# State-space stages: decays and convolution kept in PSUM, masked products on VectorE, between-block products issued together

## The chip, the cores and the metric

The kernel runs on one core of a Trainium2 chip. The core has five engines with queues of their own: TensorE (PE, matrix products into PSUM), VectorE (DVE), ScalarE (ACT, functions such as Exp and Silu), GpSimd (POOL) and SyncE (SP, which here issues transfers). The metric is the time of one execution on the device in microseconds; lower is better. Three executions before the change took 3060.55, 3071.86 and 3084.89 us.

## The reference

The program is a decoder of four layers on x of 16 rows x 128 positions x 256 features. Every layer adds three stages to x, each fed by a layer norm of x: an attention-like stage, a cross attention to a context, and a feed-forward stage. The change touches the first stage of layers 1 and 2, which are state-space stages. Cut to what matters, with L1 having 4 heads of 128 and a state of 64, L2 32 heads of 16 and a state of 128:

```python
zxbcdt = norm(x) @ W_in                      # gate z, xBC, dt
xBC = silu(causal_conv(xBC, taps=4) + bias)  # 512 + 2 * state channels
X, B, C = split(xBC)
dt = softplus(dt + dt_bias)                  # L2: clipped at 0
a = dt * -exp(A_log)                         # per position and head
G[l, s] = C[l] . B[s]
decay[l, s, h] = exp(sum of a[k, h], s < k <= l) for s <= l, else 0
y[l, h] = sum over s of G[l, s] * decay[l, s, h] * dt[s, h] * X[s, h] + D[h] * X[l, h]
y = y * silu(z)
x = x + (y * rsqrt(mean(y * y) + 1e-5) * norm_w) @ W_out
```

The reference writes the sum over s in chunks (64 positions in L1, 32 in L2), with a state carried between chunks; it is the same sum. The factor of the decay between two chunks splits into three: from s to the end of its chunk, over the chunks between, and from the start of l's chunk to l.

## The kernel before

`mamba` (line 761) computes both stages. `L1_attn` and `L2_attn` (992, 995) call it; `blocks` (767) is true for L2 alone. The 16 rows are handled in four groups of four (`NG`, `GB`).

`project(g)` (822) makes the group's projections. The channels lie on the partitions, the four rows' 512 positions beside each other. For each of six channel chunks it makes `pconv` in a PSUM bank, copies it with ACT into `xp` in SBUF (832, with three zero columns ahead of each row, set by POOL), writes the last tap and the bias with ACT into `xc` or `bc` in SBUF (834), adds the other three taps there with three DVE instructions (836), and applies Silu in place with ACT (839). It yields after every second chunk, so that its caller can interleave it. The rest of it, after the third yield, makes the gate `sz` (four chunks `pz`), `dt` with a softplus of many small DVE instructions, `a`, and in L2 the factors `xy` between chunks: three that go to the sources (already multiplied by `dt`) and one that goes to the result.

`begin(g, j)` (874) starts one row. It transposes X into `xs` with positions on the partitions, multiplies `xc` by D on POOL (881), makes `pg`, which is G, and `gm`, which is G with the causal mask (L2: with the mask inside a chunk of 32 alone). For the decays, DVE makes `rb` (894), PE sums it into `pseg`, and ACT writes its Exp to `lc` in SBUF (903): one tile of 512 columns in L1, two in L2. In L2 it goes on with the products between chunks: ACT copies G into `gf` (912); for each chunk c = 1, 2, 3, POOL makes `xw` from the 32, 64 or 96 positions before it (917), and PE multiplies the matching corner of `gf` with it into 32 partitions of the bank `poff` (923). The first 32 partitions get a product with a tile of zeros, `none` (922). DVE scales the result to `yo` (925).

`parts` (930, L2) finishes the row within chunks: POOL makes `xdp` (X times `dt`, even and odd heads apart), eight products `mt` of a decay with `gm` are made, five on DVE and three on POOL (939), PE multiplies each into `py` (946) in four columns of 32, and adds `yo` by a product with the identity (950). `whole` (953, L1) does the same with one `mt`. `gate` (961) adds to `xc` on DVE, multiplies by `sz` on POOL and squares on ACT; `out` (968) makes the mean, `rms` and the output product `po`, and adds to x.

The order is written by hand at the end of `mamba` (980 to 990) with `Pipe` (line 124), a list of work with the number of steps until it is due:

```python
for j in range(GB):
    begin(g, j, *ready[g])
    pipe.step()
    for _ in range((0, 2, 1, 9)[j]):
        next(work, None)
```

`begin` puts `parts` or `whole` two steps ahead, so a row's second half follows the `begin` of the next row; `gate` puts `out` one step ahead. Then comes a piece of the next group's projection: none in the pass of the first row, two pieces (four conv chunks) in the second, one in the third, and the rest in the fourth. The framework sets the waits and lays each engine's queue in about this order; where an instruction's operands are late in its planning, it can put later work ahead. On the chip each queue runs in the order so laid.

Tiles come from pools with a fixed number of buffers for each tag. PSUM has eight banks: four in the pool `mm` (`pconv`, `pz`, `pxy`, `pseg`, `poff`), two in `tp` (transposes, `pg`, `prms`, `po`) and two in `ac` (`py`, `pdt`).

Of the kernel before, what the change touches and what calls it, by code (L numbers as in the profile page):

```python
# [11 lines left out]
F32 = mybir.dt.float32  # L12
# [4 lines left out]
AF = mybir.ActivationFunctionType  # L17
ALU = mybir.AluOpType
# [4 lines left out]
P = 128  # L23
NB = 16
S = 128
D = 256
GB = 4
# [14 lines left out]
class Decoder:  # L42
# [718 lines left out]
    def mamba(self, L, H, N, clip):  # L761
# [3 lines left out]
        nc = self.nc  # L765
        HD, Q = 512 // H, 32
# [6 lines left out]
        with ExitStack() as es:  # L773
            pool = lambda n, b: es.enter_context(self.tc.tile_pool(name=L + n, bufs=b))
            one, ap, cv, sm, big = pool("1", 1), pool("a", 2), pool("cv", 2), pool("sm", 2), pool("big", 3)
            cw = one.tile([P, 6, 5], F32, tag="cw", name="cw")
# [11 lines left out]
            if blocks:  # L788
                g_ = nc.gpsimd
                tl = lambda n, k=P: one.tile([P, k], F32, tag=n, name=n)  # L790
                b4 = lambda t: t.rearrange("p (b i) -> p b i", b=4)

                after, upto, turn = tl("afterb"), tl("uptob"), tl("upto32", Q)
                for t, whole in ((after, self.after), (upto, self.upto)):
                    g_.affine_select(
                        out=b4(t), in_=b4(whole), pattern=[[-Q, 4], [0, Q]], compare_op=ALU.is_ge, fill=0.0, base=0,
                        channel_multiplier=1,
                    )
                    g_.affine_select(
                        out=b4(t), in_=b4(t), pattern=[[Q, 4], [0, Q]], compare_op=ALU.is_ge, fill=0.0, base=Q - 1,  # L800
                        channel_multiplier=-1,
                    )
                nc.vector.tensor_reduce(turn, upto.rearrange("p (b i) -> p i b", b=4), AX.X, ALU.add)

                rest = []
                for c in range(1, 4):
                    t = tl(f"rest{c}")
                    g_.affine_select(
                        out=t, in_=self.after, pattern=[[0, P]], compare_op=ALU.is_ge, fill=0.0, base=Q * c - 1,
                        channel_multiplier=-1,  # L810
                    )
                    rest.append(t)
                none = one.tile([Q, Q], F32, tag="none", name="none")
                g_.memset(none, 0.0)

                xds = [one.tile([P, H // 2, 64], F32, tag=f"xdp{i}", name=f"xdp{i}") for i in range(2)]
                for t in xds:
                    g_.memset(t, 0.0)
            else:
                after, upto = self.after, self.upto  # L820

            def project(g):
                xT = self.norm_T(g)
                xc = cv.tile([P, 4, GB, S], F32, tag="xc", name="xc")
                bc_ = ap.tile([P, 2, GT], F32, tag="bc", name="bc")
                for c, (at, m) in enumerate(CH):
                    pm = self.psum("pconv")
                    self.chain(pm[:m], [(w[:, k, at : at + m], xT[:, k, :]) for k in range(2)])
                    pj = pm[:m].rearrange("p (j s) -> p j s", j=GB)
                    xp = cv.tile([P, GB, S + 3], F32, tag="xp", name="xp")  # L830
                    nc.gpsimd.memset(xp[:m, :, 0:3], 0.0)
                    nc.scalar.copy(xp[:m, :, 3:], pj)
                    acc = xc[:m, c] if c < 4 else bc_[:m, c - 4, :].rearrange("p (j s) -> p j s", j=GB)
                    nc.scalar.activation(acc, pj, AF.Identity, bias=cw[:m, c, 4:5], scale=cw[:m, c, 3:4])  # L834
                    for k in range(3):
                        nc.vector.scalar_tensor_tensor(  # L836
                            acc, xp[:m, :, k : k + S], cw[:m, c, k : k + 1], acc, ALU.mult, ALU.add
                        )
                    nc.scalar.activation(acc, acc, AF.Silu)
                    if c % 2:  # L840
                        yield
                sz = ap.tile([P, 4, GT], F32, tag="sz", name="sz")
                for c in range(4):
                    pz = self.psum("pz")
                    self.chain(pz, [(wz[:, k, self.cols(c)], xT[:, k, :]) for k in range(2)])
                    nc.scalar.activation(sz[:, c, :], pz, AF.Silu)
                dt = ap.tile([P, GB, H], F32, tag="dt", name="dt")
                a = ap.tile([P, GB, H], F32, tag="a", name="a")
                flat = lambda t: t.rearrange("p j h -> p (j h)")
                pd = self.psum_a("pdt")[:, : GB * H].rearrange("p (j h) -> p j h", j=GB)  # L850
                for j in range(GB):
                    self.chain(pd[:, j, :], [(xT[:, k, self.cols(j)], w[:, k, DT : DT + H]) for k in range(2)])
                nc.vector.tensor_tensor(dt, pd, dtb.unsqueeze(1).broadcast_to([P, GB, H]), ALU.add)
                self.softplus(sm, flat(dt))
                if clip is not None:
                    nc.vector.tensor_scalar(dt, dt, clip[0], clip[1], ALU.max, ALU.min)
                nc.vector.tensor_tensor(a, dt, A.unsqueeze(1).broadcast_to([P, GB, H]), ALU.mult)
                xy = None
                if blocks:

                    px = self.psum("pxy")
                    for c in range(4):
                        nc.tensor.matmul(px[:, self.cols(c)], rest[c] if c < 3 else upto, flat(a), start=True, stop=True)
                    xy = ap.tile([P, 4, GB, H], F32, tag="xy", name="xy")
                    nc.scalar.activation(xy.rearrange("p c j h -> p (c j h)"), px, AF.Exp)
                    nc.vector.tensor_tensor(
                        xy[:, 0:3].rearrange("p c j h -> p c (j h)"), xy[:, 0:3].rearrange("p c j h -> p c (j h)"),
                        flat(dt).unsqueeze(1).broadcast_to([P, 3, GB * H]), ALU.mult,
                    )
                ready[g] = bc_, sz, xc, dt, a, xy  # L870
# [3 lines left out]
            def begin(g, j, bc_, sz, xc, dt, a, xy):  # L874
# [17 lines left out]
                for u in range(H // per):  # L892
# [6 lines left out]
                    )  # L899
                    ps = self.psum("pseg")  # L900
                    nc.tensor.matmul(ps, after, rb.rearrange("p h l -> p (h l)"), start=True, stop=True)
                    lc = big.tile([P, per, U], F32, tag="lc", name="lc", bufs=4)
                    nc.scalar.activation(lc.rearrange("p h l -> p (h l)"), ps, AF.Exp)
                    lcs.append(lc)
                if not blocks:
                    xd = sm.tile([P, 512], F32, tag="xd", name="xd")
                    nc.gpsimd.tensor_tensor(heads(xd), heads(xs), dj, ALU.mult)
                    pipe.put(2, lambda: whole(g, j, gm, lcs[0], xd, sz, xc))
                    return
                xd = xds[b % 2]  # L910
                gf = sm.tile([P, P], F32, tag="gf", name="gf")
                nc.scalar.copy(gf, pg[:, :P])
                pf = self.psum("poff")
                for c in range(1, 4):
                    n = Q * c
                    xw = big.tile([P, 512], F32, tag="xw", name="xw")
                    nc.gpsimd.tensor_tensor(
                        heads(xw)[:n], heads(xs)[:n],
                        xy[:n, c - 1, j, :].unsqueeze(2).broadcast_to([n, H, HD]), ALU.mult,
                    )  # L920
                    if c == 1:
                        nc.tensor.matmul(pf[0:Q], none, xw[0:Q], start=True, stop=True)
                    nc.tensor.matmul(pf[n : n + Q], gf[:n, n : n + Q], xw[:n], start=True, stop=True)
                yo = sm.tile([P, 512], F32, tag="yo", name="yo")
                nc.vector.tensor_tensor(
                    heads(yo), heads(pf), xy[:, 3, j, :].unsqueeze(2).broadcast_to([P, H, HD]), ALU.mult
                )
                pipe.put(2, lambda: parts(g, j, gm, lcs, xd, dj, yo, xs, sz, xc))

            def parts(g, j, gm, lcs, xd, dj, yo, xs, sz, xc):  # L930
                for e in range(2):
# [2 lines left out]
                py = self.psum_a("py")  # L934
                for c in range(4):
                    for e in range(2):
                        mt = big.tile([P, 4, 4, Q], F32, tag="mt", name="mt", bufs=3)
                        at = 8 * (c % 2) + e
                        (nc.gpsimd if e and c else nc.vector).tensor_tensor(  # L939
                            mt,  # L940
                            lcs[c // 2][:, at : at + 7 : 2, :].unsqueeze(2).broadcast_to([P, 4, 4, Q]),
                            gm.rearrange("p (b l) -> p b l", b=4).unsqueeze(1).broadcast_to([P, 4, 4, Q]),
# [40 lines left out]
            for g in range(NG):  # L983
                work = iter(project(g + 1)) if g + 1 < NG else iter(())
                for j in range(GB):
                    begin(g, j, *ready[g])
                    pipe.step()
                    for _ in range((0, 2, 1, 9)[j]):
                        next(work, None)
            pipe.drain()  # L990

    def L1_attn(self):
# [699 lines left out]
```

## Time and profile before

| | us |
|---|---|
| profiled execution | 3070.78 |
| its span on the core | 3069.1 |
| median of the three runs | 3071.86 |
| PE busy | 2517.6 (82%) |
| DVE busy | 1684.7 (55%) |
| POOL busy | 937.2 (31%) |
| ACT busy | 877.0 (29%) |

A profile is of one execution. A row of a group names line, engine and operation, the tile written and the tiles read, their shapes, and how many there were; then the busy time of the group in us and the mean of one in ns; then the idle time of the engine ahead of it and what ended it. A row of the busy table by stretches gives the stretch, its length, and the busy us of each engine with the number of instructions, then the mean granted clock of PE, the share of the transfer engines and their GB/s. A row of the timeline begins with start and length in us. A row of waits gives engine and line that waited, what it waited for, the us in total, how often, and the longest. A float32 matrix product shows as two instructions.

L1_attn fills about 643 to 840 us of the span and L2_attn about 1224 to 1625 us, with their neighbours overlapping at the edges.

### The profile page before, as it was taken

The numbers are of one execution on the slowest core, as the hardware profiler recorded it, in microseconds if no ns is written. First come the engines' busy times: TensorE is split into PE (matmuls) and PEld (weight loads), VectorE is DVE, ScalarE is ACT, GpSimd is POOL, SyncE is SP. The second block draws the span as 40 slices with busy tenths as digits, with TensorE's granted clock in tenths as the row PEclk, the third lists the DMA queues.
The fourth block names the chain that finished last, engine by engine and source line by source line (L and its number), as shares of the span: only waits on it lengthen the run. The fifth ranks groups of instructions, "written<-read, shape, count | busy, mean of one in ns | idle before, by whom it ended". The sixth has DMA issues, their size and how long they took to land. (4 is left out here: it accounts for less than half of the span.)

```text
span 3069.1 us, 33079 instructions
## 1 busy us (share of the span) xinstructions
PE 2517.6 (82%) x12524; PEld 1571.2 (51%) x12524; DVE 1684.7 (55%) x3219; ACT 877.0 (29%) x1602; POOL 937.2 (31%) x953
## 2 busy tenths in 40 slices
PE   7214998999879888889989888759998986888986
PEld 4102444556534555344445555525765565676665
DVE  6998894257643676866776666562145554211110
ACT  1002544135444311423313333221114430111111
POOL 3452111014520122444566666400023324011121
PEclk9556889999968999977889999969888985899998
DMA  4000001000100001000000000010000011132121
GB/s 121 0 0 23 24 6 42 0 31 1 39 14 1 1 1 35 4 1 1 5 20 7 1 1 1 26 42 0 24 13 1 13 54 61 51 95 64 55 75 14
DMA packets 58141, 74.33 MB, mean 24 GB/s; under 512 B 7620, under 2 KB 49669, under 8 KB 57878
## 3 DMA queue, kind: packets, MB, share of 16 engines
q1 hardware_dynamic: 50678, 63.66, 6.6%
q0 software_dynamic: 7296, 8.48, 1.5%
q8 instruction: 101, 1.65, 0.2%
q14 instruction: 66, 0.54, 0.1%
HBM read 55.12 MB, written 18.04 MB: 24 GB/s over the span
## 5 line engine op out<-in xcount | busy, mean ns | idle before, releaser
L1578 POOL DMA_INDIRECT out_dram<-y,xe x40 | 62.0, 1549 | 382.7 <-ACT y L1577 293.7
L1569 DVE TENSOR_TENSOR hT<-sl,pgb 128x320 f32<-128x320 f32 x112 | 54.6, 488 | 195.3 <-PE pgb L92 195.3
L230 PE MATMUL pt<-ident,o 128*128 128x128 f32 x64 | 18.7, 362 | 156.2 <-POOL o L298 132.7
L92 PE MATMUL pga<-xeT,e_w1T 128*128 128x320 f32 x448 | 143.2, 443 | 0.0
L92 PE MATMUL pgb<-xeT,e_w3T 128*128 128x320 f32 x448 | 139.7, 434 | 0.0
L92 PE MATMUL pa<-e_w2T,hT 128*128 128x256 f32 x560 | 125.9, 384 | 0.0
L549 DVE TENSOR_TENSOR hT<-sl,pgb 128x512 f32<-128x512 f32 (+1 forms) x56 | 38.5, 688 | 142.3 <-PE pgb L92 134.9
L92 PEld LDWEIGHTS pa<-e_w2T,hT 128*128 128x128 f32 x560 | 107.3, 193 | 14.9
L195 POOL COPY rs<-mv 128x4 f32<-128x4 f32 x48 | 11.4, 237 | 320.6 <-DVE mv L194 320.6
L1313 POOL TENSOR_TENSOR sc<-sc,mx 128x512 f32<-128x512 f32 x64 | 65.2, 1039 | 136.8 <-DVE mx L1312 99.2
L939 DVE TENSOR_TENSOR mt<-lc,gm 128x512 f32<-128x512 f32 x80 | 100.0, 1266 | 9.9 <-PE py L946 8.8
L92 PEld LDWEIGHTS pga<-xeT,e_w1T 128*128 128x128 f32 x448 | 87.3, 197 | 35.4 <-issue 1.8
L92 PEld LDWEIGHTS pgb<-xeT,e_w3T 128*128 128x128 f32 x448 | 86.0, 192 | 36.3 <-issue 1.4
L1568 ACT ACTIVATE sl<-pga 128x320 f32<-128x320 f32 x112 | 49.0, 437 | 191.3 <-PE pga L92 191.3
L270 POOL TENSOR_TENSOR prod<-qkv 128x2048 f32<-128x2048 f32 (+7 forms) x24 | 86.5, 3609 | 48.4 <-DVE o L294 28.7
L198 DVE TENSOR_SCALAR xn<-x,mv,rs 128x256 f32<-128x256 f32 x192 | 83.5, 484 | 25.6 <-POOL rs L102 25.6
L230 PEld LDWEIGHTS pt<-ident,o 128*128 128x128 f32 x64 | 9.1, 164 | 171.4 <-POOL o L298 139.8
L92 PE MATMUL pconv<-xT,w_L_w 128*128 128x512 f32 (+1 forms) x192 | 93.1, 631 | 0.7 <-ACT xT L84 0.5
L620 PE MATMUL ps<-qb,kn 32*128 32x256 f32 x512 | 88.7, 524 | 4.0 <-DVE kn L606 2.8
L382 PE MATMUL ps<-qb,kT 32*128 32x512 f32 x256 | 80.3, 714 | 13.6 <-ACT pT L387 10.4
L836 DVE SCALAR_TENSOR_TENSOR xc<-xp,cw,xc 128x512 f32<-128x512 f32 x96 | 84.1, 906 | 12.8 <-ACT xc L834 10.0
L1120 ACT ACTIVATE sc<-sc 128x512 f32<-128x512 f32 x64 | 40.3, 630 | 162.1 <-POOL sc L1119 162.1
(473 smaller groups left out, 6331.8 us busy)
## 6 DMA issues: line engine op xcount, KB each, us to landing
e_w1T<-in_L_w1T SPq DMA_DIRECT2D x8, 896.0 KB, 6.2
e_w3T<-in_L_w3T SPq DMA_DIRECT2D x8, 896.0 KB, 6.5
e_w2T<-in_L_w2T SPq DMA_DIRECT2D x8, 896.0 KB, 6.3
slots<-blank SPq DMA_DIRECT2D x8, 652.5 KB, 11.2
xe<-slots SPq DMA_DIRECT2D x8, 652.5 KB, 4.1
ct<-in_ctx SPq DMA_DIRECT2D x8, 512.0 KB, 5.4
x<-in_x SPq DMA_DIRECT2D x4, 512.0 KB, 6.2
ctx<-in_ctx SPq DMA_DIRECT2D x16, 128.0 KB, 2.2
```

The costliest lines, as they stand in the source:

```text
L92: self.nc.tensor.matmul(out, a, b, start=(i == 0), stop=(i == n - 1))
L198: nc.vector.tensor_scalar(xn[:, j, :], self.x[:, g * GB + j, :], mv[:, j, 0:1], rs[:, j : j + 1], ALU.subtract, ALU.mult)
L270: nc.gpsimd.tensor_tensor(prod[:, :k, :], qkv[:, m0 : m0 + k, 256:512], q, ALU.mult)
L382: nc.tensor.matmul(ps[r], kT[rw, j, c, :], qb[rw, j, c].rearrange("p e n -> p (e n)"), start=True, stop=True)
L620: nc.tensor.matmul(ps[r][:, D * c : D * c + D], kn[rw, j, self.cols(c)], qb[rw, j, e], start=True, stop=True)
L836: nc.vector.scalar_tensor_tensor(acc, xp[:m, :, k : k + S], cw[:m, c, k : k + 1], acc, ALU.mult, ALU.add)
L939: (nc.gpsimd if e and c else nc.vector).tensor_tensor(mt, lcs[c // 2][:, at : at + 7 : 2, :].unsqueeze(2).broadcast_to([P, 4, 4, Q]), gm.r ...
L1120: nc.scalar.activation(sc, sc, AF.Exp, scale=scale)
L1313: nc.gpsimd.tensor_tensor(sc, sc, mx.unsqueeze(2).broadcast_to([P, 4, S]), ALU.add)
L1568: nc.scalar.activation(sl, pa[:, :HALF], AF.Silu)
L1569: nc.vector.tensor_tensor(hT[:, f, hs], sl, pb[:, :HALF], ALU.mult)
L1578: nc.gpsimd.indirect_dma_start(out, bass.IndirectOffsetOnAxis(xe[:, t, D + 4 : D + 5].bitcast(I32), 0), y, None, bounds_check=NB * S - 1, ...
```

## The change

All of it is in `mamba`:

- The convolution stays in `pconv`'s PSUM bank: ACT writes the last tap and the bias there in place, DVE adds the three other taps there, and Silu alone writes `xc` or `bc` in SBUF.
- The Exp of the decays is written in place into `pseg`'s bank. There is no `lc` tile; `mt` reads the bank.
- All eight `mt` of a row in L2 are made on DVE, with five buffers instead of three.
- `gf` is made on DVE as G times a mask `prior` that is one for pairs of different chunks alone, so that the corners need not be cut: each `xw` has 96 positions (four buffers instead of three), and the four products into `poff` are issued one after the other, all with 96 rows; the first chunk's product takes the first `xw` and masked zeros. The tile `none` goes.
- `begin` returns the row's second half instead of putting it into the pipe. The loop calls it after the piece of projection of the same pass.

```diff
-                none = one.tile([Q, Q], F32, tag="none", name="none")
-                g_.memset(none, 0.0)
+                prior = tl("prior")
+                nc.vector.tensor_tensor(prior, self.upto, upto, ALU.subtract)
...
-                    acc = xc[:m, c] if c < 4 else bc_[:m, c - 4, :].rearrange("p (j s) -> p j s", j=GB)
-                    nc.scalar.activation(acc, pj, AF.Identity, bias=cw[:m, c, 4:5], scale=cw[:m, c, 3:4])
+                    nc.scalar.activation(pj, pj, AF.Identity, bias=cw[:m, c, 4:5], scale=cw[:m, c, 3:4])
                     for k in range(3):
                         nc.vector.scalar_tensor_tensor(
-                            acc, xp[:m, :, k : k + S], cw[:m, c, k : k + 1], acc, ALU.mult, ALU.add
+                            pj, xp[:m, :, k : k + S], cw[:m, c, k : k + 1], pj, ALU.mult, ALU.add
                         )
-                    nc.scalar.activation(acc, acc, AF.Silu)
+                    to = xc[:m, c] if c < 4 else bc_[:m, c - 4, :].rearrange("p (j s) -> p j s", j=GB)
+                    nc.scalar.activation(to, pj, AF.Silu)
...
-                    lc = big.tile([P, per, U], F32, tag="lc", name="lc", bufs=4)
-                    nc.scalar.activation(lc.rearrange("p h l -> p (h l)"), ps, AF.Exp)
-                    lcs.append(lc)
+                    nc.scalar.activation(ps, ps, AF.Exp)
+                    lcs.append(ps.rearrange("p (h l) -> p h l", h=per))
...
-                    pipe.put(2, lambda: whole(g, j, gm, lcs[0], xd, sz, xc))
-                    return
+                    return lambda: whole(g, j, gm, lcs[0], xd, sz, xc)
...
-                nc.scalar.copy(gf, pg[:, :P])
-                pf = self.psum("poff")
-                for c in range(1, 4):
-                    n = Q * c
-                    xw = big.tile([P, 512], F32, tag="xw", name="xw")
+                nc.vector.tensor_tensor(gf, pg[:, :P], prior, ALU.mult)
+                pf, n, xws = self.psum("poff"), 3 * Q, []
+                for c in range(3):
+                    xw = big.tile([P, 512], F32, tag="xw", name="xw", bufs=4)
                     nc.gpsimd.tensor_tensor(
-                        heads(xw)[:n], heads(xs)[:n],
-                        xy[:n, c - 1, j, :].unsqueeze(2).broadcast_to([n, H, HD]), ALU.mult,
+                        heads(xw)[:n], heads(xs)[:n], xy[:n, c, j, :].unsqueeze(2).broadcast_to([n, H, HD]), ALU.mult
                     )
-                    if c == 1:
-                        nc.tensor.matmul(pf[0:Q], none, xw[0:Q], start=True, stop=True)
-                    nc.tensor.matmul(pf[n : n + Q], gf[:n, n : n + Q], xw[:n], start=True, stop=True)
+                    xws.append(xw)
+                for c in range(4):
+                    to = slice(Q * c, Q * c + Q)
+                    nc.tensor.matmul(pf[to], gf[:n, to], xws[max(c - 1, 0)][:n], start=True, stop=True)
...
-                pipe.put(2, lambda: parts(g, j, gm, lcs, xd, dj, yo, xs, sz, xc))
+                return lambda: parts(g, j, gm, lcs, xd, dj, yo, xs, sz, xc)
...
-                        mt = big.tile([P, 4, 4, Q], F32, tag="mt", name="mt", bufs=3)
+                        mt = big.tile([P, 4, 4, Q], F32, tag="mt", name="mt", bufs=5)
                         at = 8 * (c % 2) + e
-                        (nc.gpsimd if e and c else nc.vector).tensor_tensor(
+                        nc.vector.tensor_tensor(
...
-                    begin(g, j, *ready[g])
+                    rest_of = begin(g, j, *ready[g])
                     pipe.step()
                     for _ in range((0, 2, 1, 9)[j]):
                         next(work, None)
+                    rest_of()
```

## The prediction

> **What bounds the kernel now.** The page's chain of waits covers only the last 35 us of the run, so it tells nothing here. I read the busy table by stretches first. The change touches two stages: L1_attn, whose steady part is 660 to 835 us, and L2_attn, 1256 to 1622 us.
> ```profile
> core 0: us, PE busy (x) PEld busy (x) DVE busy (x) ACT busy (x) POOL busy (x), PEclk, DMA share, GB/s
> 660.00:835.00 175.00, 160.65 (x715) 105.85 (x714) 125.45 (x269) 89.64 (x134) 72.84 (x88) 0.93 0.03 8
> 1256.00:1622.00 366.00, 327.73 (x1911) 165.55 (x1910) 263.84 (x350) 106.93 (x167) 204.25 (x197) 0.83 0.02 7
> ```
> PE is busy 90% of L2_attn and 92% of L1_attn; DMA is nothing. L2_attn has 16 batch rows at 366/16 = 22.9 us each, at a granted clock of only 0.83. So PE leads, with DVE (72%) behind. Next the groups of DVE and POOL within L2_attn, and what PE waited for:
> ```profile
> L939 DVE TENSOR_TENSOR mt<-lc,gm 128x512 f32<-128x512 f32 x80 | 100.0, 1266 | 9.9 <-PE py L946 8.8 <-DVE mt L939 0.3
> L836 DVE SCALAR_TENSOR_TENSOR xc<-xp,cw,xc 128x512 f32<-128x512 f32 x36 | 37.4, 1070 | 2.2 <-ACT xc L834 1.8
> L836 DVE SCALAR_TENSOR_TENSOR bc<-xp,cw,bc 128x512 f32<-128x512 f32 x18 | 26.6, 1497 | 1.6 <-ACT bc L834 1.6
> L925 DVE TENSOR_TENSOR yo<-poff,xy 128x512 f32<-128x512 f32 x16 | 11.0, 689 | 44.2 <-PE poff L923 44.2
> L939 POOL TENSOR_TENSOR mt<-lc,gm 128x512 f32<-128x512 f32 x48 | 68.7, 1441 | 37.6 <-PE py L946 37.4
> PE py L946 <- POOL mt L939: 17.1, 28, 1.9
> PE poff L922 <- POOL xw L917: 9.6, 8, 2.4
> ```
> All five tiles have 512 columns, yet `mt`, both inputs in SBUF, takes 1266 ns while `yo`, one input in PSUM, takes 689 (its source view: 676 to 693 over all 16). The minima of the slow ones are 670 (`mt`) and 734 (L836). The timeline shows where the rest comes from:
> ```profile
> 1390.36 7.53 DVE L836 SCALAR_TENSOR_TENSOR xc<-xp,cw,xc 128x512 f32<-128x512 f32 x4
> ...
> 1391.53 3.52 POOL L917 TENSOR_TENSOR xw<-xs,xy 32x512 f32<-32x512 f32 x3
> 1395.02 1.65 POOL L933 TENSOR_TENSOR xdp<-xs,dt 128x256 f32<-128x256 f32 x2
> ```
> Four such instructions should take 4 x 0.75 = 3 us; they took 7.5 while POOL ran. DVE's 264 us are in good part standing still.
>
> The products between blocks on PE:
> ```profile
> 1260.16 2.62 PE L923 MATMUL poff<-xw,gf 32*32 32x512 f32 x5
> 1256.00:1622.00 366.00, 70.28 (x128) 8.05 (x128) 11.03 (x16) 0.83 0.02 7
> 1383.82 0.64 PE L946 MATMUL py<-mt,xdp 128*32 128x128 f32 x16
> ```
> The second row is the stretch restricted to `poff`: 70.28 us of PE, 4.4 per row, for eight instructions (a float32 product is two). Five in 2.62 us is one after the other. Against that, sixteen `py` instructions, also 32 columns wide but all with 128 rows, take 0.64 us; one alone is 0.27, so four run side by side.
>
> **What the Trainium skill says.** "SBUF — State Buffer", section Who interferes with whom: a DVE instruction with two SBUF inputs contends with a GpSimd instruction that reads SBUF, and one with at most one SBUF input does not. The trace agrees: 1266 against 689 ns. "TensorEngine Tiling (Array Packing)", Key Properties: different tiles run in parallel, and changing the tiling mode drains TensorE. The trace agrees as far as it goes: poff with 32, 64 and 96 rows runs serially, py with one shape does not. "VectorE: DVE Perf Modes", section on the errata: a PSUM source costs 120 fixed cycles against 58. The trace disagrees for a two-input op: 689 against 682 ns (L1's SBUF `mt`, median). "TensorE: Matmul & The Clock Gate", Part 1: an idle PE falls to half clock. Here poff lasts 587 to 1062 ns, two speeds; which idle causes it, the trace doesn't say.
>
> **Part by part.**
> *Products between blocks.* The four now all have 96 rows, come in one run, and differ only in the 32 columns. By the py row I take two passes of a 512-column instruction (0.45 us from start to start at 1260 us) plus 0.16 of latency: 1.05 us, at the mixed clock about 1.3. PE: 16 x 1.3 = 21 instead of 70.3, **-49 us**. Bounds: 0 if they stay serial, -55 if all at full clock. They start after the third `xw` instead of the first; before, the third product waited for it too, so `yo` is no later. POOL's `xw` with 32 and 64 rows becomes 96: the minimum is 1046 ns at all three, so nothing.
> *gf.* From ACT (0.26 us) to DVE with a mask: 16 x 0.28 = +4.5 us of DVE, -4 of ACT. ACT's copy once stood behind two Silus (its timeline: 1399.72, ten us after `xs`), so `poff` cannot be later for this.
> *mt.* All 128 on DVE, with one PSUM input: 128 x 0.69 = 88 us against 100; POOL loses 68.7. PE's 17.1 us of waits on POOL's mt go; DVE's mt are next in line, each 0.69 for 0.13 to 0.25 us of PE, so part returns. I count nothing for it, range -17 to +10.
> *Convolution.* 54 instructions per stage in place in PSUM. No row shows one: from below `yo`'s 0.69, from above 0.75 plus 62 cycles of the skill's PSUM price, an estimate of 0.81. I take 0.75: 54 x 0.75 = 40.5 instead of 64.0 in L2_attn and of 45.9 in L1_attn. DVE: -23.5 and -5.4. ACT's Identity (0.78) and Exp (0.60) now write PSUM; no row shows that, I leave them as they are: ACT is busy 29% of the stage, and 0.1 us either way on some 50 instructions is hidden by its idle time.
> *Sum on DVE, L2_attn:* -23.5 - 12 + 4.5 = -31, to 233 of 366 us. It lies beside PE, so I count it only as slack that PE's loss can use. `rb` keeps two SBUF inputs and its 34 us.
> *PSUM banks.* Four banks serve `pconv`, `pz`, `pxy`, `pseg`, `poff`. Before, a conv bank was free after ACT's second read: 1374.5 to 1378.5, 4 us. Now it is held through the Silu: on the same chunk until 1383.6, 9.1 us, less what POOL's blocking cost. The decays hold two (L1: one) until the last `mt`. PE's next conv chunk and the next row's `pseg` queue behind these, and DVE's waits for them. More SBUF buffers (`mt` 5 instead of 3, `xw` 4) can only shorten waits. Cover: while a bank turns, PE has the row's 64 py, 8 identity, 8 prms and 8 po instructions, some 6 us per row. I take zero; without cover it is the slower rival.
> *Order.* `parts`/`whole` with all they issue (xdp, mt, py, gate's three) move from behind the next row's `begin` to behind the projection's piece; `out` comes one pass earlier. The rows of a projection's softplus now have the previous row's mt to run beside; in the pass without projection the exp to mt to py chain has prms and po (3.2 us) as cover. Zero, +-10. No DMA is added or moved, so SP's queue is untouched. The removed memset and the added mask run once, below 1 us.
> *L1_attn:* PE loses no work there. Of its 14 us idle I take 4 back for the faster convolution; range -8 to +10.
>
> Sum: -49 - 4 = -53 us. The profiled execution took 3070.8 (span 3069.1); 3070.8 - 53 = **3018 us**. The median of the runs shown is 3071.9, one us higher, so nothing is added.
>
> **Rivals.**
> *(1) PE's gain turns into idle.* The row's chain px, xs, xw on POOL, poff, yo, py, gate is as long as before, and if it sets the pace only waits that vanish count: 17 (POOL's mt) plus 4 give 3050. For it: DVE waited 44.2 us for poff, and POOL needs 3.1 us for three xw. Against: PE stands idle only 38 of 366 us, so there is little chain left uncovered.
> *(2) Too few banks: slower.* In L2_attn two banks are left for the convolution. With turn T, uncovered, each of 18 chunks costs T/2 - 1.76 (16 matmuls took 7.03 us for four chunks), and in L1_attn, three left, T/3 - 1.76. Both: 15 T - 63. It eats the 53 us at T = 7.8 us. With the 9.1 measured plus two `mt` in between, T = 10.5, the balance is +41: 3112 us. For it: DVE serves conv and mt in one queue, and a PE that waits longer may lose clock. Against: cover as above, and the 9.1 held blocked DVE time that goes.
> *(3) It does not do what it says:* DVE is still blocked with PSUM operands, or the four products stay serial. Then 3071, no change. `yo`'s 676 to 693 speaks against the first, py against the second.
>
> **How the numbers follow.** A measurement of this kernel can tell about 1% (31 us) from no change. Main case 0.66: 2985 to 3040, with the bounds -55, -17 and -8 on one side and +10 each on the other, a few hundredths below. Rivals 1 and 3 together 0.20: 3041 to 3080. Rival 2 0.14, 3080 to 3130, a small part of it within 1%. Range 2980 to 3072: it leaves out most of rival 2 and some hundredths at the bottom. Faster 0.66, same 0.21, slower 0.13.
>
> **What would show it.** Right: poff's PE share of L2_attn near 20 us, the stage near 315; DVE's mt at 690 and L836's successor at 690 to 810 with no long ones; POOL without mt. Wrong: DVE idle on pconv or PE on a Silu (banks), clock below 0.8 in L2_attn, poff at 50 us or more.

## The result and the profile after

The changed kernel takes 3050.3 us (median of 12 runs, 3038.5 to 3073.2) against 3073.5 (12 runs) before: a ratio of 0.9924, with a 95% interval of 0.9901 to 0.9946. That is 23 us less, where 53 were forecast: the right way, under half the size.

Where the time went is read from the two stages. A stage's length here runs from its first `pconv` product to its last addition to x. First the busy table by stretches for the kernel before, over these lengths, then the same for the changed kernel (columns as before):

```profile
core 0: us, PE busy (x) PEld busy (x) DVE busy (x) ACT busy (x) POOL busy (x), PEclk, DMA share, GB/s
642.50:837.20 194.70, 179.72 (x760) 114.01 (x760) 141.25 (x295) 102.52 (x155) 76.21 (x99) 0.94 0.03 9
1222.50:1622.00 399.50, 353.04 (x1997) 179.02 (x1998) 293.09 (x407) 124.19 (x197) 215.43 (x218) 0.84 0.03 9
```

```profile
650.50:866.30 215.80, 191.34 (x760) 123.24 (x760) 131.73 (x295) 111.70 (x163) 71.70 (x99) 0.90 0.03 8
1247.40:1599.50 352.10, 309.93 (x2020) 175.07 (x2022) 246.79 (x475) 126.05 (x185) 130.20 (x169) 0.87 0.04 11
```

L2_attn fell by 47.4 us, close to the 49 forecast. L1_attn, forecast at -4, grew by 21.1, with the same 760 PE instructions: PE stood idle 24.5 us instead of 15.0, and the same work took 191.3 us instead of 179.7, at a clock of 0.90 instead of 0.94. Net -26.3; the two medians differ by 23. (The profiled execution itself took 3058.6, since the stages that the change doesn't touch were 14 us longer in it than in the one before. The experiments are therefore read from the stages: the six kernels with the changed kernel's L2_attn show 350.0 to 352.3 us.)

The prices of DVE came out as forecast. The groups of DVE in the changed kernel's L2_attn (line, engine, operation, tiles, shapes and count; busy us and mean ns; idle time ahead and its releasers):

```profile
L937 DVE TENSOR_TENSOR mt<-pseg,gm 128x512 f32<-128x512 f32 x128 | 83.1, 682 | 3.1 <-PE py L944 2.0 <-ACT pseg L903 0.6
L836 DVE SCALAR_TENSOR_TENSOR pconv<-xp,cw,pconv 128x512 f32<-128x512 f32 x72 | 51.0, 750 | 8.3 <-ACT pconv L834 7.8 <-issue 0.5
L895 DVE TENSOR_TENSOR rb<-upto,a 128x512 f32<-128x512 f32 x32 | 37.4, 1197 | 1.3 <-PE pseg L902 1.3
```

With one input in PSUM, `mt` takes 682 ns (1266 before; forecast 690) and the convolution 750 (989 for `xc` and 1311 for `bc` before, over the whole stage; forecast 750). `rb`, both inputs in SBUF, still takes 1197. The products between blocks took 35.7 us of PE instead of 70.3 (forecast 21); this row is the L2_attn stretch restricted to `poff`:

```profile
1242.00:1600.00 358.00, 35.73 (x128) 5.61 (x128) 11.04 (x16) 0.87 0.04 10
```

And this is what PE waited for in the changed kernel's L1_attn, the longest first (waiter, releaser, total us, times, longest):

```profile
PE prms L92 <- ACT sz L963: 19.1, 10, 2.8
PE py L956 <- DVE mt L953: 1.9, 2, 1.5
```

`prms` is the first product of `out`, and `sz L963` the Square that ends `gate`. Before, that wait was 1.2 us in the stage. One of the ten in the timeline of the changed kernel (start, length in us):

```profile
724.65 1.06 PE L956 MATMUL py<-mt,xd 128*128 128x128 f32 x8
...
725.63 0.49 PE L886 MATMUL pg<-bc 64*128 64x128 f32 x2
725.74 0.69 DVE L961 TENSOR_TENSOR xc<-xc,py 128x512 f32<-128x512 f32 x1 [0.17 <-PE py L956]
...
726.89 1.26 POOL L962 TENSOR_TENSOR xc<-xc,sz 128x512 f32<-128x512 f32 x1
...
728.18 0.63 ACT L963 ACTIVATE sz<-xc 128x512 f32<-128x512 f32 x1 [4.37 <-POOL xc L962]
...
728.87 1.05 PE L92 MATMUL prms<-ones,sz 128*128 128x1 f32 x8 [2.75 <-ACT sz L963]
```

After `py` the row passes DVE, POOL and ACT, some 3 us, before `prms` may start. PE has only the next row's `pg` in between, and then stands idle for 2.75 us.

### The profile page after: what moved, and what is told of

Read it like the earlier page. It is cut to its first block, busy times and chain, and to the rows that moved or that the text cites. A ratio compares the mean times of both kernels' runs of the same rounds, so it can differ in the third digit from the quotient of the medians.

```text
span 3056.8 us, 33106 instructions
## 1 busy us (share of the span) xinstructions
PE 2495.4 (82%) x12524; PEld 1581.7 (52%) x12524; DVE 1630.6 (53%) x3284; ACT 886.7 (29%) x1598; POOL 846.8 (28%) x904
## 5 line engine op out<-in xcount | busy, mean ns | idle before, releaser
L1568 DVE TENSOR_TENSOR hT<-sl,pgb 128x320 f32<-128x320 f32 x112 | 54.6, 488 | 194.6 <-PE pgb L92 194.6
L836 DVE SCALAR_TENSOR_TENSOR pconv<-xp,cw,pconv 128x512 f32<-128x512 f32 (+1 forms) x144 | 103.0, 750 | 15.4 <-ACT pconv L834 14.0
L382 PE MATMUL ps<-qb,kT 32*128 32x512 f32 x256 | 86.1, 764 | 13.8 <-ACT pT L387 10.0
L92 PE MATMUL po<-w_L_woT,xc 128*128 128x256 f32 x256 | 94.2, 532 | 0.0
```

Of the source, the lines that this page charges most:

```text
L92: self.nc.tensor.matmul(out, a, b, start=(i == 0), stop=(i == n - 1))
L382: nc.tensor.matmul(ps[r], kT[rw, j, c, :], qb[rw, j, c].rearrange("p e n -> p (e n)"), start=True, stop=True)
L836: nc.vector.scalar_tensor_tensor(pj, xp[:m, :, k : k + S], cw[:m, c, k : k + 1], pj, ALU.mult, ALU.add)
L1568: nc.vector.tensor_tensor(hT[:, f, hs], sl, pb[:, :HALF], ALU.mult)
```

## The experiments

The lengths of the two stages, in us, each from one profiled execution. Where the code of a stage is the same in several kernels, the lengths agree within 0.4 us in L1_attn (174.5 in seven kernels) and within 2.3 us in L2_attn:

| kernel | L1_attn | L2_attn |
|---|---|---|
| before | 194.7 | 399.5 |
| changed | 215.8 | 352.1 |
| l1_as_before | 194.3 | 352.3 |
| l1_conv_sbuf | 223.0 | 352.2 |
| l1_decay_sbuf | 226.8 | 350.0 |
| l1_old_order | 174.5 | 352.2 |
| l1_out_later | 179.9 | 350.0 |
| x_poff_old | 174.5 | 373.4 |
| poff_only | 194.6 | 364.3 |
| x_conv_sbuf | 174.5 | 343.2 |
| x_decay_sbuf | 174.5 | 334.4 |
| x_both_sbuf | 174.5 | 359.3 |
| x_decay_pool | 174.5 | 363.6 |
| x_decay_old_order | 174.5 | 299.9 |
| y_conv_sbuf | 194.3 | 333.2 |
| y_mt_pool | 188.3 | 334.3 |

**l1_as_before.** The edits shown under the next two headings (l1_conv_sbuf with l1_decay_sbuf, and l1_old_order) together: L1_attn as it was.

> The changed kernel, with L1_attn entirely as before (order, convolution and decays) and L2_attn as changed. The stage's length is taken from the first pconv to the last addition to x: L1_attn 194.7 us before and 215.8 changed, L2_attn 399.5 and 352.1. If the loss sits in L1_attn and the gain in L2_attn, and the two are independent, L1_attn is back at 195 +-4 and L2_attn stays at 352 +-5, and the whole is some 21 us below the changed kernel: a ratio to before near 0.985. If the loss elsewhere is what ate the gain, L1_attn alone does not bring it back, and the ratio stays near 0.992.

L1_attn 194.3, L2_attn 352.3; 3032.8 us, ratio 0.9832 (0.9807 to 0.9857). The net loss sits in L1_attn, the net gain in L2_attn, and they are independent.

**l1_conv_sbuf and l1_decay_sbuf.**

```diff
-                    nc.scalar.activation(pj, pj, AF.Identity, bias=cw[:m, c, 4:5], scale=cw[:m, c, 3:4])
+                    acc = to if not blocks else pj
+                    nc.scalar.activation(acc, pj, AF.Identity, bias=cw[:m, c, 4:5], scale=cw[:m, c, 3:4])
```

```diff
+                    if not blocks:
+                        lc = big.tile([P, per, U], F32, tag="lc", name="lc", bufs=4)
+                        nc.scalar.activation(lc.rearrange("p h l -> p (h l)"), ps, AF.Exp)
+                        lcs.append(lc)
+                    else:
+                        nc.scalar.activation(ps, ps, AF.Exp)
+                        lcs.append(ps.rearrange("p (h l) -> p h l", h=per))
```

Here `to` is the tile in SBUF, `xc` or `bc`; the three taps and the Silu, not shown, use `acc` in place of `pj`.

> The changed kernel, but L1_attn's convolution is accumulated in SBUF as before, so that its bank is free after ACT's two reads; order and decays as changed. Bank theory: L1_attn near 195 to 200 us. Order theory: it stays near 212 to 220.

> The changed kernel, but L1_attn's decays go to SBUF as before; order and convolution as changed. If the one bank that the decays hold is the cost, L1_attn is near 195 to 200 us. Order theory and convolution-bank theory both: 210 to 218.

223.0 and 226.8 us: both longer than 215.8 (ratios to before 0.9933 and 1.0021). Neither bank explains the loss in L1_attn; even in the changed order, keeping these in PSUM gains 7 and 11 us.

**l1_old_order.**

```diff
                     rest_of = begin(g, j, *ready[g])
+                    if not blocks:
+                        pipe.put(2, rest_of)
                     pipe.step()
                     for _ in range((0, 2, 1, 9)[j]):
                         next(work, None)
-                    rest_of()
+                    if blocks:
+                        rest_of()
```

> The changed kernel, but L1_attn's second half (whole) goes back into the pipe, two steps ahead; its convolution and decays stay in PSUM. Order theory (the second half right behind its own begin leaves the chain from mt to prms uncovered): L1_attn near 195 to 200 us. Bank theory (the convolution holds its bank through the Silu): L1_attn stays near 216 or gets longer, since the decays now hold a bank for two passes.

It fell below both ends that were expected. The stage in the busy table of this kernel:

```profile
646.30:820.80 174.50, 169.42 (x760) 107.46 (x760) 130.31 (x295) 110.56 (x163) 72.43 (x99) 1.00 0.03 10
```

and PE's longest waits in it:

```profile
PE pz L92 <- ACT xc L840: 1.1, 1, 1.1
...
PE prms L92 <- ACT sz L963: 0.2, 1, 0.2
```

The 19.1 us of waiting for the Square are 0.2. PE's idle time fell from 24.5 to 5.1 us and its busy time, for the same 760 instructions, from 191.3 to 169.4, with the clock at 1.00. So the new order alone costs L1_attn 41.3 us: 19.4 of standing still and 21.9 of slower running. The whole takes 3007.6 us, ratio 0.9738 (0.9697 to 0.9779).

The slower running is in the clock records of the traces. In L1_attn they grant PE either the full clock or half of it: nine stretches at half clock in the changed kernel, none in l1_old_order. PE worked for 42.2 us of these stretches, which costs it 21.1 us. The same sum for the kernel before gives 10.4 us, and its PE was busy 10.3 us longer than in l1_old_order. The busy table of the changed kernel shows one such stretch in its second row; the wait of 2.75 us in the timeline above lies in the first:

```profile
724.60:731.00 6.40, 3.65 (x26) 3.21 (x25) 3.03 (x8) 0.63 (x1) 4.41 (x7) 1.00 0.01 3
731.10:734.50 3.40, 3.40 (x15) 3.07 (x14) 1.20 (x4) 0.59 (x1) 0.65 (x1) 0.51 0.00 0
```

All seven of the waits for the Square that last more than 1 us are followed by a stretch at half clock, within 2.3 us of their end. The other two stretches, at 758 and 810 us, follow no wait of PE above 0.3 us in the 29 us ahead of them.

**l1_out_later.** Which distance matters, from `begin` to `whole` or from `gate` to `out`?

```diff
-                pipe.put(1, lambda: out(g, j, y, sq))
+                pipe.put(2 if not blocks else 1, lambda: out(g, j, y, sq))
```

> The changed kernel with one number changed for L1_attn: gate puts out two steps ahead instead of one. whole still follows its own begin in the same pass. In the changed kernel's L1_attn PE waited 19.1 us in 10 waits, and its weight loads 24.5 us, for the Square that ends gate. If that short distance from gate to prms is the loss, these waits go and L1_attn falls from 215.8 to below 195 us with a clock near 1. If the distance from begin to whole is the loss, it stays above 205.

179.9 us at a clock of 0.99, with the second half still in the pass of its own `begin`. The distance from `gate` to `out` was 35.9 of the 41.3 us.

**x_poff_old and poff_only.** The prediction's largest term, taken away from a kernel with the changed L2_attn (its L1_attn as in l1_old_order), and put alone into the kernel before. The edit is the hunk of the diff that begins with `gf`, with `prior` and `none`.

> l1_old_order (L1_attn 174.5 us, L2_attn 352.2) with L2_attn's products between blocks as before: gf copied by ACT, 32, 64 and 96 rows, the tile of zeros, each product behind its own xw. All else as changed. The prediction's largest term, -49 us, says that L2_attn gets 45 to 50 us longer, near 400. By poff's measured fall, from 70.3 to 35.7 us of PE, it is 35, near 387. If these products lie beside other work, it stays below 365.

> The kernel before with one part alone: gf on DVE with the mask, 96 rows, the four products together; L1_attn and all else as before. The prediction's term says L2_attn falls from 399.5 by 45 to 50 us, to 350 to 355. By x_poff_old against l1_old_order it is 21 us: 378. If POOL's chain (xw, mt) sets the pace there, PE's gain turns to idle and it stays above 388.

21.2 and 35.2 us, not 49. In poff_only `poff` still takes 47.1 us of PE, and 35.7 in the changed kernel. The timeline of the changed kernel shows why this is more than the forecast 21. The fences show PE at a row at 1443 us; POOL's `xw`, first the last one of another row and then all three of the row at 1443; and PE at that other row, at 1290 us.

```profile
1443.70 4.39 PE L921 MATMUL poff<-xw,gf 96*32 96x512 f32 x8 [1.92 <-POOL xw L915]
```

```profile
1284.91 1.05 POOL L915 TENSOR_TENSOR xw<-xs,xy 96x512 f32<-96x512 f32 x1
...
1442.14 3.99 POOL L915 TENSOR_TENSOR xw<-xs,xy 96x512 f32<-96x512 f32 x3
```

```profile
1290.04 1.06 PE L921 MATMUL poff<-xw,gf 96*32 96x512 f32 x8
```

At 1290 all three `xw` were done (the last at 1286), and the eight instructions ran side by side in 1.06 us, as forecast. At 1443 the first product started as the first `xw` landed, and the later ones as theirs did: the run stretched over POOL's 3 us. They stand together in PE's queue, but each still waits for its own `xw`. In 7 of the 16 rows of the changed kernel, and in 13 of poff_only, the first product started before the last `xw` had landed.

**x_conv_sbuf, x_decay_sbuf, x_both_sbuf, x_decay_pool.** From here L1_attn is that of l1_old_order. The first two are the edits of l1_conv_sbuf and l1_decay_sbuf with the condition `blocks`; the third is both; the fourth is x_decay_sbuf with

```diff
-                        nc.vector.tensor_tensor(
+                        (nc.gpsimd if e and c else nc.vector).tensor_tensor(
```

for `mt`.

> l1_old_order with L2_attn's convolution accumulated in SBUF as before. If DVE's blocked time there was slack, as the prediction counted it, L2_attn stays at 352 +-4. If the convolution's bank is what PE now waits for, it gets shorter. If DVE's time is on the path, it gets longer by up to the 23 us that DVE lost to POOL there before, less now that POOL makes no mt.

> l1_old_order with L2_attn's decays written to SBUF as before, so that all 128 mt of DVE have two inputs in SBUF. If those wait for POOL as before (1266 ns on average), DVE gets 75 us more work and L2_attn 20 to 60 us more. Since POOL now only has xw, xdp and the gate's products, some of the mt run free: then the mean lies near 900 ns and the stage within 15 us of 352.

> x_decay_sbuf with L2_attn's convolution in SBUF too, so that nothing of L2_attn stays in PSUM longer than before; all mt on DVE, the products between blocks together, the order as changed. If scarce banks are what PSUM costs in L2_attn, freeing the convolution's banks adds to freeing the decays' and L2_attn is at 322 to 332 us. If two free banks more are enough, the convolution in PSUM is the better one for DVE and L2_attn is at 336 to 345.

> x_decay_sbuf with three of the eight mt of a row on POOL, as before the change. If the move of mt from POOL is what gained (17.1 us of PE waiting for POOL's mt before, and DVE blocked by POOL), L2_attn gets 20 to 40 us longer than 334.4. If PE's shorter poff was all, it stays within 8 us.

Decays back in SBUF made L2_attn 17.8 us shorter (334.4), although `mt` again had two inputs in SBUF; taking the convolution back alone made it 9.0 shorter (343.2). But both back made it 7 longer than the changed kernel (359.3): the convolution in PSUM gains 24.9 us with the decays in SBUF and loses 9.0 with them in PSUM. That suggests that the two compete for the four banks, two of which hold one row's decays, but it is argued and not shown. PE's waits in the changed kernel's L2_attn, and then in that of x_decay_sbuf (cut to those named here):

```profile
PE prms L92 <- ACT sz L963: 14.3, 9, 1.8
...
PE pz L92 <- ACT xc L840: 3.6, 1, 3.6
PE pconv L92 <- DVE mt L937: 2.2, 2, 1.1
```

```profile
PE pseg L902 <- DVE rb L895: 6.1, 3, 3.1
PE prms L92 <- ACT sz L968: 5.6, 6, 1.5
PE py L949 <- POOL xdp L936: 5.5, 6, 1.7
```

`pz` behind a Silu and `pconv` behind an `mt` are waits for the last reader of a bank: 5.8 us in all, against 3.6 (all of `pz`) in x_decay_sbuf. What grew most is the wait for the Square, from 5.6 to 14.3, and the clock fell from 0.92 to 0.87. Whether scarce banks delay the chain to the Square, or the order in which the framework then lays the queues, stays open. (x_both_sbuf in full: 3012.4 us, ratio 0.9837, 0.9793 to 0.9881.) `mt` back on POOL costs 29.2 us (363.6).

**x_decay_old_order.** Both edits of order and decays: `pipe.put(2, rest_of)` for both stages, and the decays of L2_attn in four SBUF tiles.

> x_decay_sbuf (decays of L2_attn in SBUF, L2_attn 334.4 us, L1_attn 174.5) with parts put into the pipe two steps ahead too, as before the change; four decay tiles in SBUF hold two rows. If the new order costs L2_attn what it cost L1_attn (41 us of 16 rows, with a wait for the Square), L2_attn falls to 300 to 320 us. In x_decay_sbuf PE waited only 5.6 us for that Square, so with parts long enough to cover itself the order is worth nothing here: 330 to 340.

L2_attn 299.9 us; 2952.1 in all, ratio 0.9627 (0.9585 to 0.9670), the fastest kernel here. The stage in the busy table, and its `mt`:

```profile
1196.50:1496.40 299.90, 281.13 (x2024) 153.10 (x2026) 257.15 (x475) 125.20 (x186) 145.52 (x169) 0.98 0.04 12
```

```profile
L942 DVE TENSOR_TENSOR mt<-lc,gm 128x512 f32<-128x512 f32 x128 | 107.4, 880 | 0.2 <-PE py L949 0.2
```

So the order costs L2_attn 34.5 us too, though the expectation gave equal room to its costing nothing. But the wait for the Square is only a third of it here: PE's idle time fell by 15.3 us, and the waits of x_decay_sbuf for `rb`, the Square and `xdp` (17.2 us, shown above) are down to 0.4. The clock rose from 0.92 to 0.98. `mt` is blocked at times (880 ns on average) and DVE is 10 us busier than in the changed kernel, yet the stage is 52 us shorter: DVE's time was not what bounded the changed kernel's stage. The old order with the decays of L2_attn in PSUM was not tried: two rows of them hold four banks, and `poff` needs a fifth.

**y_conv_sbuf and y_mt_pool.** What of x_decay_old_order makes the gain that is left?

> x_decay_old_order (both stages in the old order, L1_attn 174.5 us, L2_attn 299.9) with the convolution accumulated in SBUF in both stages. If DVE's blocked time in the convolution was on the path, L1_attn returns to 185 to 195 us and L2_attn to 310 to 325. If the gain came from mt's move in L2_attn and from the decays in L1_attn, both stay within 5 us.

> x_decay_old_order with three of eight mt of L2_attn on POOL and L1_attn's decays in SBUF. If POOL's mt were the bulk of the gain, L2_attn returns to 335 to 360 us; if the convolution was, it stays below 315. L1_attn: its mt has one input per row only (0.69 us), so 175 to 182 if the convolution was the gain there, 185 to 195 if the decays were.

The convolution in PSUM: 33.3 us in L2_attn and 19.8 in L1_attn. `mt` off POOL: 34.4 in L2_attn. Decays in PSUM: 13.8 in L1_attn. These are not additive: in L1_attn taking back the convolution alone loses nearly all that both gained. In L2_attn PE stood idle 18.8 us in x_decay_old_order, 34.4 in y_conv_sbuf and 36.3 in y_mt_pool. In y_conv_sbuf it waited 18.8 us for DVE's `gf`, `a` and `mt`, where x_decay_old_order shows 1.3; in y_mt_pool 11.0 for `a` and `gf` of DVE and only 5.5 for POOL's `mt`. DVE's convolution in y_conv_sbuf, and its `mt` in y_mt_pool, blocked as before the change:

```profile
L838 DVE SCALAR_TENSOR_TENSOR xc<-xp,cw,xc 128x512 f32<-128x512 f32 x48 | 40.4, 884 | 2.3 <-ACT xc L836 2.2
L838 DVE SCALAR_TENSOR_TENSOR bc<-xp,cw,bc 128x512 f32<-128x512 f32 x24 | 29.0, 1241 | 0.6 <-ACT bc L836 0.5
```

```profile
L942 DVE TENSOR_TENSOR mt<-lc,gm 128x512 f32<-128x512 f32 x80 | 96.5, 1238 | 2.2 <-PE py L949 2.0 <-issue 0.2
```

## Why the prediction was wrong

**The step that failed** is *Order*: "Zero, +-10". It argued from the distance between `begin` and `whole`, whose exp to mt to py chain it found covered by `prms` and `po`. It overlooked that `prms` itself is the end of another chain, and that the same edit shortens that one: `out` "comes one pass earlier", as the prediction says, but not what then stands between `gate` and `out`. Before, there was a piece of the projection and a `begin`; now a `begin` alone. The cover named for one wait was the thing that waited. The new order cost L1_attn 41.3 us, 35.9 of which l1_out_later won back by the distance from `gate` to `out` alone. It cost L2_attn 34.5 us, with the decays in SBUF; there waits for `rb` and `xdp` came with the one for the Square.

*L1_attn, -4*: +21.1. By parts: convolution and decays in PSUM -20.2 (194.7 to 174.5), order +41.3. The gain was five times what was counted, so a change that kept the order would have been well worth it.

*L2_attn, -49*: -47.4, right only in sum, by luck. Taken in this order, since the parts are not additive, the runs give from 399.5: products together -35.2 (poff_only), convolution in PSUM and `mt` on DVE -64.4 more, order +34.5 (x_decay_old_order to x_decay_sbuf), decays in PSUM +17.7 (x_decay_sbuf to the changed kernel).

*Products between blocks, -49*: mis-sized. The stage fell by 35.2 us with them in the kernel before and by 21.2 with the rest of L2_attn as changed, and their PE time to 47.1 and 35.7 us, not 21. Side by side in 1.06 us holds where the operands are there. "They start after the third `xw`" does not: often they start one by one. (The lower bound should read -53.5: sixteen times 1.05 us leave 16.8 of 70.3.)

*DVE's 31 us as slack, POOL's 17 us at nothing*: wrong. With the old order, the convolution's share of DVE's time and `mt` off POOL were worth 33 to 34 us each. PE leads, but its idle time grew by 15.6 and 17.5 us without them, mostly for DVE, and its clock fell from 0.98 to 0.93 and 0.91.

*Prices of DVE*: right, 682 for 690 and 750 for 750 ns; the upper end, 810, from the Trainium skill's PSUM price ("VectorE: DVE Perf Modes", the section on the errata) was not needed: the traces show no such surcharge, since the same instruction with both inputs in SBUF has a median of 747 ns in x_conv_sbuf. That one PSUM input frees DVE from POOL was right (628 to 694 ns over all 128 `mt`).

*PSUM banks, zero*: right in effect for L1_attn, where convolution and decays in PSUM gain; in L2_attn the decays in PSUM cost 17.7 us with the convolution there too. Scarce banks, the mechanism of rival 2, may be the cause, in one stage and at a smaller price, but the waits don't show it.

*Rival 1* gave 3050, the number that came out, for another reason: PE's gain did not turn to idle in L2_attn, whose idle time fell from 46.5 to 42.2 us; the net loss was in L1_attn, of which the rival didn't speak.

The prediction had the clock as one of the things it could not see. The Trainium skill, "TensorE: Matmul & The Clock Gate", Part 1, says that PE loses clock after an idle window of about 3.4 us. The runs of L1_attn agree that waits cost clock, but not on the length: the longest wait in the changed kernel's L1_attn was 2.8 us, and all seven waits for the Square of 1.3 us or more were followed by a stretch at half clock. The sum of idle time doesn't set the clock: l1_conv_sbuf stood idle 32.5 us in L1_attn at a clock of 0.90, the changed kernel 24.5 at the same clock, and in L2_attn x_decay_pool stood 53.6 us at 0.90 and the changed kernel 42.2 at 0.87. Which waits lower it stays open.

## What to carry to other kernels

When a step is moved in a software pipeline, list every producer and consumer pair whose distance it changes, not only the pair that the edit is about; and if one wait is covered by another product, ask what that product waits for. On a PE that leads, look at the clock too, since a new wait can cost more than its length: here 19 us of waiting made 41, and over the pairs of kernels compared above that differ in their waits and not in PE's work, each us more of PE's idle time came with 0.9 to 3.1 us of stage. Judge parts of a change one by one: this one held 120 us of gains in its two stages (20 and 100) and gave back 94, all but 18 of it through the order of the work.

## What was not expected of the hardware

The same 760 PE instructions took 169.4 us at a granted clock of 1.00 and 191.3 at 0.90: 19 us of waits, none above 2.8 us, came with 21.9 us of slower running, in stretches at half clock of 3.4 to 6.9 us. A DVE instruction with one operand in PSUM showed no trace of POOL's work over 128 instances (628 to 694 ns), where `rb` of the same size, with both in SBUF, averaged 1197. Four 32-column products of equal shape ran fully side by side on 512 columns (1.06 us for eight instructions), but only where nothing between them waited; otherwise up to 4.39 us.
